# Spreading one operand of the graph-attention edge scores by DMA through DRAM instead of by matmuls, with the written order of one block changed to match

## Chip, cores and metric

The kernel runs on one core of a Trainium2 chip. The metric is device time in microseconds (us) of one launch, taken as the median of repeated runs. Beside it stands one profiled execution, whose trace and page are quoted here.

## What is computed

The input is 128 graphs of 128 nodes with 256 features each, and an adjacency matrix of zeros and ones for each graph. Layer 0 is a transformer layer with 8 heads, in which the attention probabilities are multiplied by value projections that depend on the edge's type. Layer 1 is two rounds of graph attention and a feed-forward block. All is in fp32.

```python
# layer 0
attn = softmax(q k^T / sqrt(32)); out = sum_r (attn * (adj == r)) @ v_r
x = LN(x + out @ Wo);  x = LN(x + gelu(x @ W1) @ W2)
# layer 1, twice _gat, then a feed-forward block
Wh  = h @ W;  Wh1 = Wh @ a[:F];  Wh2 = Wh @ a[F:]
e   = leaky_relu(Wh1 + transpose(Wh2))            # one number per pair of nodes
att = softmax(where(adj > 0, e, -9e15), axis=1);  h = att @ Wh
x = LN(x + h);  x = LN(x + relu(x @ w_ff1) @ w_ff2)
```

## The kernel before

The work is cut into 32 groups of four graphs (G = 4, 512 tokens). Everything of a group stays in SBUF. All weights are loaded once. A group goes through these stages; the names are those of the tiles in the profile.

- `projections`: `pq` gives q and k of the group (four steps), `pv` the values of each graph (four steps). ScalarE copies `qT` and `kT` out of PSUM, VectorE adds the bias to `v`.
- `attention`: `scores` computes `ps`, ScalarE takes Exp into `e`, VectorE masks it into `pm`; `attended` computes the denominators `pden` and the weighted values `pav`, and VectorE divides; then two output products `pwo`, each added to the residual by VectorE. A generator of five steps: scores 0; attended 0 with scores 1; attended 1; `pwo` 0; `pwo` 1.
- `ffn`: eight steps `ph` (two matmuls of 512 columns each, ScalarE applies Gelu or Relu into `hT`), then eight steps of `po` (eight matmuls of 256 columns each), sixteen steps in all. `first_ffn` belongs to layer 0, `second_ffn` to layer 1.
- `layer1`: the two rounds of graph attention. `pw` multiplies the group's input by `wu`, which holds W1 times W2 (256 columns) and the columns that give the score parts; ScalarE copies it to `wh`. The other score part has to stand along the free dimension on all 128 partitions. It is made there by a matmul with a weight of identical columns: `wb` in the first round (L480), and `wh`'s column D+1 broadcast to 128 columns in the second (L491). `edges` adds the two parts on ScalarE (L448, the `gs` activations with the column as bias), applies leaky relu on VectorE (L451), Exp on ScalarE (L452), the mask with its sums (L455), the reciprocal, and the division on GpSimd (L462). `py` is the first product with the scores, `pg2` (shown as `pg` in the profile) the second.
- `norm` is a layer norm (statistics and normalisation on VectorE, the power -1/2 and the scale and shift on GpSimd), `turned` transposes its result on TensorE (`pt`) and ScalarE copies it out to `yT`, `written` is the last norm and the output DMA.

Stages of three groups are interleaved by hand. `in_order(ffn_, *steps)` walks through its list: a number runs that many steps of the feed-forward block, a generator runs its next step, a function is called; what is left of the block runs at the end. In the loop over g there are two such lists: the first around `first_ffn` of group g+1 holds the beginning of `layer1` of group g; the second around `second_ffn` of group g holds the end of `layer1`, the projections and attention of group g+2, and the transposes. TensorE executes in the order written (`manual_schedule`). The order on the other engines is chosen by the scheduler when the kernel is built.

PSUM has eight buffers of 128x512: four in the pool `ps_s` (shared in turn by `ps`, `pt`, `pw`, `py` and `pg`), one each for `av` and `den`, two in `ps_mm` (`pq`, `pv`, `ph`, `po`, `pwo`). All loads of the loop and the output go through the DMA queue of SyncE (SP), in order.

Of the kernel before, what the change touches and what calls it, by code (L numbers as in the profile page):

```python
# [9 lines left out]
F32 = mybir.dt.float32  # L10
I32 = mybir.dt.int32
AF = mybir.ActivationFunctionType
# [11 lines left out]
P = 128  # L24
G = 4
T = G * P
# [77 lines left out]
def fast_pass(ctx, tc, a, out):  # L104
# [19 lines left out]
    w3p = ctx.enter_context(tc.tile_pool(name="work3", bufs=3))  # L124
    w1p = ctx.enter_context(tc.tile_pool(name="work1", bufs=1))
    small = ctx.enter_context(tc.tile_pool(name="small", bufs=4))
    ps_s = ctx.enter_context(tc.tile_pool(name="ps_s", bufs=4, space=PSUM))
    ps_av = ctx.enter_context(tc.tile_pool(name="ps_av", bufs=1, space=PSUM))
    ps_mm = ctx.enter_context(tc.tile_pool(name="ps_mm", bufs=2, space=PSUM))
# [69 lines left out]

    NU = D + 3
    wu = k.tile([P, NCH, NU], "wu")
    wb = k.tile([P, NCH, P], "wb")

    def graph_weights():

        scr = cut(D)
        wa1 = k.columns(gw1, a1, scr, "1")
        wa2 = k.columns(gw2, a2, scr, "2")  # L210
        rhs = cut(NCH, D + 2)
        nc.vector.tensor_copy(rhs[:, :, :D], gw2)
        nc.vector.tensor_copy(rhs[:, :, D : D + 1], wa2[:, :, 1:2])
        nc.vector.tensor_copy(rhs[:, :, D + 1 : D + 2], wa2[:, :, 0:1])
        gw1T = cut(NCH, D)
        for m in range(NCH):
            pt = mm_tile(f"pgt_{m}")
            for c in range(NCH):
                nc.tensor.transpose(
                    pt[:, c * P : (c + 1) * P], gw1[:, c, m * P : (m + 1) * P], k.ident  # L220
                )
            nc.scalar.copy(gw1T[:, m, :], pt[:, :D])
        yield
        for m in range(NCH):
            pu = mm_tile(f"pgw_{m}")
            for c in range(NCH):
                nc.tensor.matmul(
                    pu[:, : D + 2], gw1T[:, c, m * P : (m + 1) * P], rhs[:, c, :],
                    start=(c == 0), stop=(c == NCH - 1),
                )  # L230
            nc.scalar.copy(wu[:, m, : D + 2], pu[:, : D + 2])
            nc.vector.tensor_copy(wu[:, m, D + 2 :], wa1[:, m, 1:2])
            nc.vector.tensor_copy(wb[:, m, :], wa1[:, m, 0:1].to_broadcast([P, P]))

# [205 lines left out]
            added(t, p, po, S["xr"])  # L440
            yield

    def edges(pb, bias, S, l):

        n = f"{S['g']}_{l}"
        s = w2p.tile([P, G, P], F32, tag="gs", name="gs_" + n)
        for b in range(G):
            nc.scalar.activation(  # L448
                s[:, b, :], pb[:, b * P : (b + 1) * P], AF.Identity, bias=bias(b)
            )  # L450
        nc.vector.scalar_tensor_tensor(s, s, ALPHA, s, op0=ALU.mult, op1=ALU.max)  # L451
        nc.scalar.activation(s, s, AF.Exp)  # L452
        den = c_gat[:, S["g"], l, :]
        for b in range(G):
            nc.vector.scalar_tensor_tensor(  # L455
                s[:, b, :], s[:, b, :], 1.0, S["ad"][:, b, :],
                op0=ALU.mult, op1=ALU.mult, accum_out=den[:, b : b + 1],
            )
        rd = small.tile([P, G], F32, tag="gr", name="gr_" + n)
        nc.vector.tensor_scalar(rd, den, LO, None, op0=ALU.max)  # L460
        nc.vector.reciprocal(rd, rd)  # L461
        nc.gpsimd.tensor_mul(s, s, rd[:, :, None].to_broadcast([P, G, P]))  # L462
        return s

    def layer1(S):


        n, yT = str(S["g"]), S["x2T"]
        wh = w1p.tile([P, G, NU], F32, tag="wh", name="wh_" + n)
        for b in range(G):  # L470
            pw = ps_s.tile([P, T], F32, tag="s", name=f"pw_{n}_{b}")
            for c in range(NCH):
                nc.tensor.matmul(  # L473
                    pw[:, :NU], yT[:, c, b * P : (b + 1) * P], wu[:, c, :],
                    start=(c == 0), stop=(c == NCH - 1),
                )
            nc.scalar.copy(wh[:, b, :], pw[:, :NU])
        pb = ps_av.tile([P, T], F32, tag="den", name="pb_" + n)
        for c in range(NCH):
            nc.tensor.matmul(pb, wb[:, c, :], yT[:, c, :], start=(c == 0), stop=(c == NCH - 1))  # L480
        att = edges(pb, lambda b: wh[:, b, D + 2 : D + 3], S, 0)
        yield
        yh = w1p.tile([P, G, D + 1], F32, tag="yh", name="yh_" + n)
        pb = ps_av.tile([P, T], F32, tag="av", name="pb2_" + n)
        for b in range(G):
            py = ps_s.tile([P, T], F32, tag="s", name=f"py_{n}_{b}")
            nc.tensor.matmul(  # L487
                py[:, : D + 1], att[:, b, :], wh[:, b, : D + 1], start=True, stop=True
            )
            nc.scalar.copy(yh[:, b, :], py[:, : D + 1])  # L490
            nc.tensor.matmul(  # L491
                pb[:, b * P : (b + 1) * P], wh[:, b, D + 1 : D + 2].to_broadcast([P, P]),
                att[:, b, :], start=True, stop=True,
            )
        att = edges(pb, lambda b: yh[:, b, D : D + 1], S, 1)
        yield
        S["t2"] = t = w3p.tile([P, G, D], F32, tag="t", name="t_2_" + n)
        for p in range(G // 2):
            po = ps_s.tile([P, T], F32, tag="s", name=f"pg2_{n}_{p}")
            for s in range(2):  # L500
                b = 2 * p + s
                nc.tensor.matmul(  # L502
                    po[:, s * D : (s + 1) * D], att[:, b, :], yh[:, b, :D], start=True, stop=True
                )
            added(t, p, po, S["res1"])
        yield
# [44 lines left out]
    def first_ffn(S):  # L551
        yield from ffn(S, 1, S["x1T"], w1, b1, AF.Gelu, w2, S["res0"])

    def second_ffn(S):
        yield from ffn(S, 3, S["x3T"], u1, c1, AF.Relu, u2, S["res2"])
# [6 lines left out]

    with tc.manual_schedule(engines={mybir.EngineType.PE}):
        st = [first, entered(1)] + [None] * (NG - 2)
        none, steps = iter(()), graph_weights()
        at = attention(first)
        in_order(none, *[projections(first)] * 8, at, steps, at, steps, at, at, at)
        norm(first, 0)  # L570
        turned(first, 0)
        pr, at = projections(st[1]), attention(st[1])
        in_order(
            first_ffn(first), *[pr, 1] * 8, at, 2, at, 2, at, 2, at, at, lambda: norm(st[1], 0), 2
        )
        norm(first, 1)
        turned(st[1], 0)
        for g in range(NG - 1):
            S, S1 = st[g], st[g + 1]
            graph = layer1(S)  # L580
            if g + 2 < NG:
                st[g + 2] = S2 = entered(g + 2)
                if g == 0:
                    head = (4, lambda: turned(S, 1), 2)
                else:
                    head = (6,)
                in_order(
                    first_ffn(S1),
                    *(() if g == 0 else (lambda: written(st[g - 1]),)),
                    *head, graph, 6, graph, 4,  # L590
                )
                pr, at = projections(S2), attention(S2)
                norm(S1, 1, 0)
                in_order(
                    second_ffn(S), pr, pr, graph, lambda: norm(S, 2), lambda: norm(S1, 1, 1),
                    *[pr] * 6, lambda: turned(S1, 1), lambda: turned(S, 2),
                    at, 3, at, 3, at, 3, at, at, lambda: norm(S2, 0), 6, lambda: turned(S2, 0),
                )
            else:
                in_order(  # L600
                    first_ffn(S1), lambda: written(st[g - 1]),
                    graph, 5, graph, 5, graph, lambda: norm(S, 2), 5, lambda: turned(S, 2),
                )
                graph = layer1(S1)
                norm(S1, 1)
                in_order(
                    second_ffn(S), 4, lambda: turned(S1, 1), 1, graph, 5, graph, 5, graph,
                    lambda: norm(S1, 2),
                )
                written(S)  # L610
                turned(S1, 2)
                in_order(second_ffn(S1))
                written_by_graph(S1)
# [356 lines left out]
```

## Time and profile before

| | |
|---|---|
| median of 3 runs | 3107.01 us (3105.93 to 3108.55) |
| profiled execution | 3106.48 us, span 3104.7 us, granted TensorE clock 0.997 |
| TensorE busy | 3038.4 us (98%) |
| VectorE, ScalarE, GpSimd busy | 1349.4, 1077.0, 866.9 us |
| DMA | 69.59 MB, mean 22 GB/s |
| one group in the steady part | 95.67 us |

A row of a timeline gives the start and the length in us, the engine, the source line, the operation, the output and inputs by their names in the program, the shapes and the number of instructions; in brackets stands the idle time before it and what ended it. A matmul in fp32 has two records. Records of matmuls overlap, so a length is longer than the time until the next can start. A DMA row gives the number of issues, the size of each, and the median time from issue to landing. PE is TensorE, DVE VectorE, ACT ScalarE, POOL GpSimd.

### The profile page before, as it was taken

The page shows a single profiled execution, that of the slowest core. Times are in us where ns is not written, and L with a number is a line of the kernel's source. Part 1 is how long each engine was busy: PE and PEld are TensorE (multiplying, and loading weights), DVE is VectorE, ACT ScalarE, POOL GpSimd, SP SyncE. Part 2 cuts the span into 40 slices and gives each one's busy share as a digit, 9 for nine tenths or more (in the row PEclk, how much of TensorE's full clock was granted, in tenths as well). Part 3 has the DMA queues.
Part 4 walks back from the last instruction along what each step waited for, and adds up shares of the span by engine and source line. Part 5 has one row for each costly group of instructions (what it writes and reads, how often), then busy time and mean ns, then how long its engine had stood idle before and what let it go on. Part 6 is the DMA issues. An engine that isn't in the chain of part 4 may idle for free.

```text
span 3104.7 us, 39594 instructions
## 1 busy us (share of the span) xinstructions
PE 3038.4 (98%) x16526; PEld 1996.7 (64%) x16526; DVE 1349.4 (43%) x3445; ACT 1077.0 (35%) x1797; POOL 866.9 (28%) x489
## 2 busy tenths in 40 slices
PE   8999999999999999999999999999999999999998
PEld 4666666666666666666666666666666666666665
DVE  4544434444434454344444444443445434454443
ACT  2333343333433333333334333343333333333332
POOL 1223233232232322323313223223232232332322
PEclk9999999999999999999999999999999999999999
DMA  5000000000000000000000000000000000000000
GB/s 164 12 21 21 21 18 19 22 22 18 18 24 18 21 18 18 24 18 21 18 24 18 18 21 24 18 18 24 18 21 18 18 24 18 21 18 11 7 8 15
DMA packets 58137, 69.59 MB, mean 22 GB/s; under 512 B 6752, under 2 KB 44768, under 8 KB 57952
## 3 DMA queue, kind: packets, MB, share of 16 engines
q1 hardware_dynamic: 57120, 66.61, 7.0%
q8 instruction: 131, 2.15, 0.3%
q14 instruction: 54, 0.44, 0.0%
q10 hardware_dynamic: 832, 0.40, 0.0%
HBM read 50.22 MB, written 16.78 MB: 22 GB/s over the span
## 4 chain that ended last, share of the span: by engine, by line
PE 94%; ACT 3%; DVE 1%; DMA 1%; POOL 0%; SPq 0%; issue 0%; ACTq 0%; DVEq 0%; POOLq 0%
PE po L308 29%; PE ph L296 28%; PE pq L402 7%; PE pv L412 7%; PE pwo L436 4%; PE pw L473 4%; PE pav L372 3%; ACT yT L278 3%; PE ps L342 2%; PE pden L363 2%; PE py L487 2%; PE pb L480 2%; PE pg L502 2%; PE pt L275 2%; PE pb L491 1%; DVE t L285 1%
## 5 line engine op out<-in xcount | busy, mean ns | idle before, releaser
L255 POOL TENSOR_TENSOR rs<-rs,mhalf 128x4 f32<-128x4 f32 x127 | 128.9, 1015 | 1298.3 <-DVE rs L254 1298.2
L296 PE MATMUL ph<-yT,w_L_gnn_w_ff 128*128 128x512 f32 x1024 | 466.1, 603 | 0.0
L308 PE MATMUL po<-w_L_gnn_W,hT 128*128 128x256 f32 x2048 | 460.9, 381 | 1.3 <-ACT hT L300 1.3
L308 PE MATMUL po<-w_L_gnn_w_ff,hT 128*128 128x256 f32 x2048 | 457.5, 379 | 0.0
L296 PE MATMUL ph<-yT,w_L_gnn_W 128*128 128x512 f32 x1024 | 451.6, 592 | 2.4 <-ACT hT L300 2.0
L308 PEld LDWEIGHTS po<-w_L_gnn_W,hT 128*128 128x128 f32 x2048 | 384.0, 190 | 76.3 <-issue 14.5
L308 PEld LDWEIGHTS po<-w_L_gnn_w_ff,hT 128*128 128x128 f32 x2048 | 386.7, 190 | 65.1 <-issue 14.8
L296 PEld LDWEIGHTS ph<-yT,w_L_gnn_W 128*128 128x128 f32 x1024 | 194.2, 190 | 234.3 <-issue 219.8
L278 ACT ACTIVATE yT<-pt,c_L_gnn_beta,c_L_gnn_g 128x512 f32<-128x512 f32 x128 | 92.6, 773 | 721.6 <-PE pt L275 721.5
L296 PEld LDWEIGHTS ph<-yT,w_L_gnn_w_ff 128*128 128x128 f32 x1024 | 187.7, 190 | 215.2 <-issue 192.4
L285 DVE TENSOR_TENSOR t<-po,res 128x512 f32<-128x512 f32 x128 | 88.5, 691 | 445.7 <-PE po L308 445.7
L379 DVE RECIPROCAL rd<-pden 128x512 f32<-128x512 f32 x64 | 214.9, 3357 | 153.4 <-PE pden L363 153.3
L300 ACT ACTIVATE hT<-ph,c_L_gnn_b_ff 128x512 f32<-128x512 f32 x256 | 176.3, 689 | 291.9 <-PE ph L296 290.2
L462 POOL TENSOR_TENSOR gs<-gs,gr 128x512 f32<-128x512 f32 x64 | 66.5, 1039 | 724.1 <-DVE gr L461 712.9
L300 ACT ACTIVATE hT<-ph,c_L_gnn_b 128x512 f32<-128x512 f32 x256 | 175.7, 687 | 219.2 <-PE ph L296 218.7
L412 PE MATMUL pv<-wv,xT 128*128 128x512 f32 x512 | 225.4, 592 | 0.0
L451 DVE SCALAR_TENSOR_TENSOR gs<-gs 128x512 f32<-128x512 f32 x64 | 44.6, 697 | 412.9 <-ACT gs L448 412.8
L350 DVE TENSOR_TENSOR pm<-e,adj 128x512 f32<-128x512 f32 x256 | 159.5, 685 | 130.5 <-ACT e L349 130.5
L251 DVE BATCH_NORM_STATS2 st<-t 128x6 f32<-128x256 f32 x508 | 192.3, 415 | 7.4
L257 DVE TENSOR_SCALAR t<-t,mv,rs 128x256 f32<-128x256 f32 x384 | 132.6, 409 | 112.5 <-POOL rs L255 112.5
L349 ACT ACTIVATE e<-ps 128x512 f32<-128x512 f32 x256 | 132.1, 603 | 140.5 <-PE ps L342 140.5
L412 PEld LDWEIGHTS pv<-wv,xT 128*128 128x128 f32 x512 | 97.3, 190 | 122.4 <-issue 122.2
(110 smaller groups left out, 3772.1 us busy)
## 6 DMA issues: line engine op xcount, KB each, us to landing
xT<-in_xT_dram SPq DMA_DIRECT2D x32, 512.0 KB, 3.6
x<-in_x_dram SPq DMA_DIRECT2D x32, 512.0 KB, 3.9
out_dram<-t SPq DMA_DIRECT2D x31, 512.0 KB, 2.9
adj<-in_adjT_dram SPq DMA_DIRECT2D x32, 256.0 KB, 2.7
w_L_gnn_W<-in_L_gnn_W_dram SPq DMA_DIRECT2D x2, 1024.0 KB, 7.6
w_L_gnn_w_ff<-in_L_gnn_w_ff_dram SPq DMA_DIRECT2D x2, 1024.0 KB, 9.9
wv<-in_L_gnn_Wv_dram SPq DMA_DIRECT2D x2, 256.0 KB, 5.3
temp<-in_L_gnn_W_dram SPq DMA_DIRECT2D x2, 256.0 KB, 4.9
```

The lines of the kernel that those rows point to most:

```text
L251: nc.vector.bn_stats(st[:, b, :], t[:, b, :])
L255: nc.gpsimd.tensor_tensor(rs, rs, k.mhalf, op=ALU.pow)
L257: nc.vector.tensor_scalar(t[:, b, :], t[:, b, :], mv[:, b, 0:1], rs[:, b : b + 1], op0=ALU.subtract, op1=ALU.mult,)
L278: nc.scalar.activation(yT[:, c, :], pt, AF.Identity, bias=bc[:, c : c + 1], scale=gc[:, c : c + 1])
L296: nc.tensor.matmul(ph, wa[:, c, f * P : (f + 1) * P], inT[:, c, :], start=(c == 0), stop=(c == NCH - 1),)
L300: nc.scalar.activation(hT[:, f, :], ph, func, bias=ba[:, f : f + 1])
L308: nc.tensor.matmul(po[:, s * D : (s + 1) * D], hT[:, f, b * P : (b + 1) * P], wb_[:, f, :], start=(f == 0), stop=(f == NF - 1),)
L349: nc.scalar.activation(e[:, s], pss[s], AF.Exp, scale=SCALE)
L350: nc.vector.tensor_mul(pm[:, s], e[:, s], ad[:, 2 * p : 2 * p + 2, None, :].to_broadcast([P, 2, NCH, P]),)
L379: nc.vector.reciprocal(rd, pden)
L402: nc.tensor.matmul(pq, w[:, c, m * P : (m + 1) * P], xt[:, c, :], start=(c == 0), stop=(c == NCH - 1),)
L412: nc.tensor.matmul(pv, xt[:, c, b * P : (b + 1) * P], wv[:, c].rearrange("p r d -> p (r d)"), start=(c == 0), stop=(c == NCH - 1),)
```

## The change

The broadcast matmuls L480 and L491 and the tile `wb` are removed. `wu` gets a fourth extra column, so that `pw` delivers both score parts as columns of `wh`, and `py` delivers both as columns of `yh`. A new function `spread` takes one column per graph (128 partitions x 4), writes it by DMA to a small DRAM tile `line` (four rows of 128 numbers), and reads it back by a second DMA into all 128 partitions, as the SBUF tile `pb` (128x512). Both DMAs go on SP's queue. `edges` reads `pb` from SBUF.

`layer1` now has five steps instead of three: `pw` with the first transfer; edges 0; `py` with the second transfer; edges 1; `pg2`. The lists of `in_order` put feed-forward steps or projections between them. In the second list the transposes `turned(S1, 1)` and `turned(S, 2)`, which stood together ahead of scores 0, are put one v product ahead of them and two v products behind them, and one `ph` step stands between the two `pwo`. ScalarE is added to the engines that execute in written order.

```diff
-    NU = D + 3
+    NU = D + 4
     wu = k.tile([P, NCH, NU], "wu")
-    wb = k.tile([P, NCH, P], "wb")
...
-            nc.vector.tensor_copy(wb[:, m, :], wa1[:, m, 0:1].to_broadcast([P, P]))
+            nc.vector.tensor_copy(wu[:, m, D + 2 : D + 3], wa1[:, m, 1:2])
+            nc.vector.tensor_copy(wu[:, m, D + 3 :], wa1[:, m, 0:1])
...
+    def spread(column, n):
+        line = dram.tile([G, P], F32, tag="line", name="line_" + n)
+        with nc.allow_non_contiguous_dma(reason="a column per graph as a row"):
+            nc.sync.dma_start(line.rearrange("b p -> p b"), column)
+        pb = w2p.tile([P, G, P], F32, tag="pb", name="pb_" + n)
+        nc.sync.dma_start(pb, line.partition_broadcast(P))
+        return pb
...
-        pb = ps_av.tile([P, T], F32, tag="den", name="pb_" + n)
-        for c in range(NCH):
-            nc.tensor.matmul(pb, wb[:, c, :], yT[:, c, :], start=(c == 0), stop=(c == NCH - 1))
-        att = edges(pb, lambda b: wh[:, b, D + 2 : D + 3], S, 0)
+        target = spread(wh[:, :, D + 3], n + "_0")
         yield
-        yh = w1p.tile([P, G, D + 1], F32, tag="yh", name="yh_" + n)
-        pb = ps_av.tile([P, T], F32, tag="av", name="pb2_" + n)
+        att = edges(target, wh[:, :, D + 2 : D + 3], S, 0)
+        yield
+        yh = w1p.tile([P, G, D + 2], F32, tag="yh", name="yh_" + n)
         for b in range(G):
...
-            nc.tensor.matmul(
-                pb[:, b * P : (b + 1) * P], wh[:, b, D + 1 : D + 2].to_broadcast([P, P]),
-                att[:, b, :], start=True, stop=True,
-            )
-        att = edges(pb, lambda b: yh[:, b, D : D + 1], S, 1)
+            nc.scalar.copy(yh[:, b, :], py[:, : D + 2])
+        target = spread(yh[:, :, D + 1], n + "_1")
+        yield
+        att = edges(target, yh[:, :, D : D + 1], S, 1)
         yield
...
-    with tc.manual_schedule(engines={mybir.EngineType.PE}):
+    with tc.manual_schedule(engines={mybir.EngineType.PE, mybir.EngineType.Activation}):
...
                 else:
-                    head = (6,)
+                    head = (1,)
                 in_order(
                     first_ffn(S1),
                     *(() if g == 0 else (lambda: written(st[g - 1]),)),
-                    *head, graph, 6, graph, 4,
+                    *head, graph, 7, graph, 4, graph, 4,
                 )
...
                 in_order(
-                    second_ffn(S), pr, pr, graph, lambda: norm(S, 2), lambda: norm(S1, 1, 1),
-                    *[pr] * 6, lambda: turned(S1, 1), lambda: turned(S, 2),
-                    at, 3, at, 3, at, 3, at, at, lambda: norm(S2, 0), 6, lambda: turned(S2, 0),
+                    second_ffn(S), graph, *[pr] * 4, graph, lambda: norm(S, 2), lambda: norm(S1, 1, 1),
+                    pr, lambda: turned(S1, 1), pr,
+                    at, pr, pr, lambda: turned(S, 2),
+                    at, 4, at, 3, at, 1, at, lambda: norm(S2, 0), 6, lambda: turned(S2, 0),
                 )
...
                 in_order(
                     first_ffn(S1), lambda: written(st[g - 1]),
-                    graph, 5, graph, 5, graph, lambda: norm(S, 2), 5, lambda: turned(S, 2),
+                    graph, 3, graph, 3, graph, 3, graph, 3, graph, lambda: norm(S, 2),
+                    4, lambda: turned(S, 2),
                 )
...
                 in_order(
-                    second_ffn(S), 4, lambda: turned(S1, 1), 1, graph, 5, graph, 5, graph,
+                    second_ffn(S), 4, lambda: turned(S1, 1), 1,
+                    graph, 3, graph, 3, graph, 3, graph, 2, graph,
                     lambda: norm(S1, 2),
                 )
```

More of the change, by code (lines that the diff above doesn't have):

```diff
@@ L126, in fast_pass @@
     small = ctx.enter_context(tc.tile_pool(name="small", bufs=4))
+    dram = ctx.enter_context(tc.tile_pool(name="dram", bufs=2, space=bass.MemoryType.DRAM))
     ps_s = ctx.enter_context(tc.tile_pool(name="ps_s", bufs=4, space=PSUM))
@@ L231, in graph_weights @@
             nc.scalar.copy(wu[:, m, : D + 2], pu[:, : D + 2])
-            nc.vector.tensor_copy(wu[:, m, D + 2 :], wa1[:, m, 1:2])
-            nc.vector.tensor_copy(wb[:, m, :], wa1[:, m, 0:1].to_broadcast([P, P]))
+            nc.vector.tensor_copy(wu[:, m, D + 2 : D + 3], wa1[:, m, 1:2])
+            nc.vector.tensor_copy(wu[:, m, D + 3 :], wa1[:, m, 0:1])
     c_adj = k.tile([P, NG], "c_adj")
@@ L441, in attention, with edges @@
             yield
-    def edges(pb, bias, S, l):
+    def spread(column, n):
[5 more added lines that the diff above has]
+        return pb
+    def edges(target, source, S, l):
         n = f"{S['g']}_{l}"
@@ L448, in edges @@
             nc.scalar.activation(
-                s[:, b, :], pb[:, b * P : (b + 1) * P], AF.Identity, bias=bias(b)
+                s[:, b, :], target[:, b, :], AF.Identity, bias=source[:, b, :]
             )
@@ L487, in layer1 @@
             nc.tensor.matmul(
-                py[:, : D + 1], att[:, b, :], wh[:, b, : D + 1], start=True, stop=True
+                py[:, : D + 2], att[:, b, :], wh[:, b, : D + 2], start=True, stop=True
             )
-            nc.scalar.copy(yh[:, b, :], py[:, : D + 1])
-            nc.tensor.matmul(
-                pb[:, b * P : (b + 1) * P], wh[:, b, D + 1 : D + 2].to_broadcast([P, P]),
-                att[:, b, :], start=True, stop=True,
-            )
-        att = edges(pb, lambda b: yh[:, b, D : D + 1], S, 1)
+            nc.scalar.copy(yh[:, b, :], py[:, : D + 2])
+        target = spread(yh[:, :, D + 1], n + "_1")
+        yield
+        att = edges(target, yh[:, :, D : D + 1], S, 1)
         yield
@@ L573, in fast_pass @@
         in_order(
-            first_ffn(first), *[pr, 1] * 8, at, 2, at, 2, at, 2, at, at, lambda: norm(st[1], 0), 2
+            first_ffn(first), *[pr, 1] * 8, at, 2, at, 2, at, 2, at, 1, at, lambda: norm(st[1], 0), 1
         )
@@ L583, in fast_pass @@
                 if g == 0:
-                    head = (4, lambda: turned(S, 1), 2)
+                    head = (4, lambda: turned(S, 1), 1)
                 else:
-                    head = (6,)
+                    head = (1,)
                 in_order(
```

## Prediction

> **What bounds the kernel now.** I read the busy shares first, then the chain that ended last, then the timeline of one steady group (it repeats every 95.67 us: the 48-matmul stretch of L308 starts at 190.40, 286.07, 381.75).
>
> ```profile
> PE 3038.4 (98%) x16526; PEld 1996.7 (64%) x16526; DVE 1349.4 (43%) x3445; ACT 1077.0 (35%) x1797; POOL 866.9 (28%) x489
> PE 94%; ACT 3%; DVE 1%; DMA 1%; POOL 0%; SPq 0%; issue 0%; ACTq 0%; DVEq 0%; POOLq 0%
> ```
>
> TensorE is both the busiest engine and 94% of the chain, so an instruction that leaves its queue shortens the run by its start-to-start time, and an edit elsewhere counts only where TensorE comes to wait. The timeline of TensorE shows what the change touches (start, length, group):
>
> ```profile
> 1019.70 1.91 PE L275 MATMUL pt<-ident,t 128*128 128x128 f32 x16
> 1021.54 0.78 PE L342 MATMUL ps<-qT,kT 32*128 32x128 f32 x4
> 1022.50 0.48 PE L342 MATMUL ps<-qT,kT 32*128 32x128 f32 x2 [0.18 <-ACT yT L278]
> 1023.17 1.15 PE L342 MATMUL ps<-qT,kT 32*128 32x128 f32 x26 [0.18 <-ACT yT L278]
> 1024.26 5.42 PE L296 MATMUL ph<-yT,w_L_gnn_w_ff 128*128 128x512 f32 x12
> ...
> 1046.80 1.89 PE L436 MATMUL pwo<-w_L_gnn_Wo,oT 128*128 128x256 f32 x8
> 1049.48 1.99 PE L436 MATMUL pwo<-w_L_gnn_Wo,oT 128*128 128x256 f32 x8 [0.78 <-DVE t L285]
> ...
> 1078.07 1.88 PE L480 MATMUL pb<-yT,wb 128*128 128x512 f32 x4
> 1079.79 3.60 PE L296 MATMUL ph<-yT,w_L_gnn_W 128*128 128x512 f32 x8
> ...
> 1090.81 0.38 PE L491 MATMUL pb<-gs,wh 128*128 128x128 f32 x2
> 1091.03 0.60 PE L487 MATMUL py<-wh,gs 128*128 128x257 f32 x2
> ```
>
> Records overlap, so I use differences of starts, not lengths. The score matmuls take 2.72 us (1021.54 to 1024.26) although the other batch of the same 32 takes 1.10 (1032.35 to 1033.45): they wait for the PSUM buffers of the transposes just ahead, which ScalarE is still emptying. The chain gives that stretch to "ACT yT L278", 2.79 us, so the printed 0.18 understates it.
>
> The cover for the new transfers is judged by these rows:
>
> ```profile
> adj<-in_adjT_dram SPq DMA_DIRECT2D x32, 256.0 KB, 2.7
> out_dram<-t SPq DMA_DIRECT2D x4, 128.0 KB, 1.8
> 1073.81 0.38 SPq L527 DMA_DIRECT2D out_dram<-t  x1
> 1093.28 1.14 ACT L448 ACTIVATE gs<-pb,yh 128x128 f32<-128x128 f32 x4
> 1095.73 0.63 ACT L452 ACTIVATE gs<-gs 128x512 f32<-128x512 f32 x1
> 1097.89 1.04 POOL L462 TENSOR_TENSOR gs<-gs,gr 128x512 f32<-128x512 f32 x1 [10.98 <-DVE gr L461]
> ```
>
> The last three are one edge chain: 5.65 us from the first gs to the normalised scores (1093.28 to 1098.93), with a table load of 1.28 inside.
>
> [...] 4-byte packets of the column loads at the start take 8 to 9 ns each, and some 1,084 of them pass in 1.9 us. [...]
>
> **The change, part by part** (per steady group unless said).
>
> (a) Broadcast matmuls removed: L480, 1079.79-1078.07 = 1.72 us; L491, four times 1091.03-1090.81 = 0.22, 0.88. In all 2.60 x 32 groups = -83.2 us. wb's copies (0.4 us in all) were hidden anyway.
>
> (b) One more column in pw (259 to 260) and py (257 to 258): 24 records at 0.43 us per 512 columns, under 1 ns each: 0.02 us a group, +0.6.
>
> (c) Transposes away from the scores: two v products now follow scores 0, and turned(S, 2) comes after them. The transposes of turned(S1, 1) have one v product (1.72 us) between them and scores 0; ScalarE's two copies end about 1.3 us after the last transpose (773 ns each). The wait of 2.72-1.10 = 1.62 goes, 30 groups: -48.6. If the cover failed it would be the same 1.62 again.
>
> (d) pwo: one ph product now stands between its halves. Before, the second half started 2.68 us after the first instead of 1.73; -0.95 x 31 = -29.5. The next one late would be DVE's add (0.69 + 0.2), inside 1.72.
>
> (e) ScalarE in written order, edges after the last hT: Gelu's table is no longer swapped out amid hT. "PEld po L308 <- ACT hT L300" is 14.2 us over 32 waits; its effect on starts is 7.16 against 6.91 us per 32 records, -0.25 x 31 = -7.7.
>
> (f) First transfer. Take t = 0 at the group's first ph. pw ends at 5.2 (ph 1.72, four pw 3.50), the last wh copy at 5.8 (0.2 behind it, 0.38 long). SP's queue has the output write of the group before ahead of it, issued 9.5 us after that ph (1073.81-1064.27); so the line goes at 9.95, lands about a microsecond behind those 512 KB (2.9 from issue), at 13.5, and the broadcast 2.7 later, at about 16.3. gs stands behind the last hT (ph ends at 5.2+7 x 1.717 = 17.2, then 0.2+0.69), at 18.05: 1.7 us of slack. Scores ready at 18.05+5.65 = 23.7; py is due at 17.2 + 4 steps of 1.73 = 24.1. Cost 0, slack 0.4; without that cover the trip costs what it passes 8.1 by. Behind the waiting gs stand Exp and the yh copies, which nothing needs before py. The wh copies also wait for the last group's line to be read, long done.
>
> (g) Second transfer. py ends (call it 0), yh at 0.6. Trip D: the write 2.3 (1.8 of the 128 KB row, plus 512 pieces at 1.9/1084), the broadcast 2.7 (adj's row: same 128 packets of 2 KB), 0.1 between: D = 5.1. Bounds: 4.5 (1.8 + 2.7), and 7 if 4-byte writes cost twice the reads and 128 reads of one 2 KB row slow the broadcast. gs starts at 0.6+D, takes 1.15. On DVE the normalisation of t1 is queued between the masked sums and the reciprocal (order of instructions in the changed kernel) and waits for POOL's power: leaky relu and Exp 1.4, sums and statistics 1.7, power 1.13 (rs to L257), normalisation 1.38, reciprocal 0.45, POOL's product 1.2, hand-over 0.1 make 7.35 us from the last gs to the scores on TensorE, so ready at 9.1+D. TensorE gets to pg at 13.8 (4 po steps 6.9, four q/k products 6.87). Slack is 4.7-D = -0.4: about 0.5 x 30 = +15 (0 to 70). Behind gs on ScalarE stand Exp and the q copies; these hold up the third q/k product only from D = 6.5.
>
> (h) SP: adj, xT, x come behind these four issues; they wait for releases at about 39, 51 and 76 us anyway and are used a group or more later. 0. DVE and POOL get no work. ScalarE reads its gs from SBUF instead of PSUM, the same 128 columns: 0.
>
> (i) Last two groups: only three ffn steps (5.2 us) lie between graph stages, and in group 31's turn the read-back stands behind an output write. Edges block hT there: in group 30 gs can start at about 14, and Exp and the reload of Gelu put the fourth hT at 18.6, where TensorE wants its buffer at 12.1 (6.5); pg then waits some 2.4, and in group 31 py 0.7 and pg 3.5. Less the 1.96 and 1.29 that ph and po wait there now: +10 (0 to 20).
>
> Sum: -83.2+0.6-48.6-29.5-7.7+15+10 = -143. From the profiled run's 3106.5 us (span 3104.7), which lies 0.5 below the median of 3107.0: **2963**. The group would go from 95.67 to some 90.8.
>
> **Rivals.**
> 1. Two round trips do not fit. In both stages DMA becomes the wait. Second stage costs D-4.7, first D-8.1; (a) to (e) less (i) give about 5.3 per group, so it turns slower where (D-4.7)+(D-8.1) passes 5.3: **D = 9**. At D = 12 it is +11.2-5.3 = 5.9 x 30: about 3280. Against it: no steady transfer of 256 or 512 KB takes over 3.9 us; for it: column loads at the crowded start took up to 9.3, and 4-byte writes to DRAM are nowhere in the trace.
> 2. The trip is late by some more (D 6 to 8), or small slacks of 0.3 to 0.5 us (scores 0, py, v's PSUM) fail: 1 to 4 us a group come back, 3000 to 3080.
> 3. The moves do nothing, as another buffer is late in place of (c) and (d): only (a) is left less the trip, -83+25: about 3050.
>
> **How the numbers follow.** Forecast 0.57 (range 2940 to 2995); rivals 2 and 3 together 0.31; rival 1 0.10; the rest about no change. A measurement of this kernel can tell 0.2% (6 us) from nothing. Faster 0.87, same 0.03, slower 0.10. The range must reach into rivals 2 and 3: 2935 to 3065 leaves out rival 1, the upper end of 2, and a little below.
>
> **What would show it.** Right: no row pb<- on PE, TensorE busy down by about 80 us, ps after pv at 1.1 us a batch, no pwo wait, period near 90.8, pg waiting a few tenths for POOL. Wrong: "ACT gs <- DMA pb" followed by PE waiting for POOL gs by microseconds a group (rival 1 or 2); ps or pwo still waiting (rival 3). The landing times of line and pb give D directly; a line write of over 4 us would break the forecast.

## The result, and the profile after

The changed kernel takes 3756.4 us (median of 4 runs, 3754.34 to 3758.12) against 3107.66 (3105.93 to 3108.55): a ratio of 1.2088, with an interval of 1.2067 to 1.2109. It is 21% slower. The forecast was 2963, so the result lies on the other side of no change and outside the range. The profiled execution has a span of 3752.5 us and a granted TensorE clock of 0.911.

The busy shares of the changed kernel, and the shares of its chain by engine:

```profile
PE 3153.6 (84%) x16142; PEld 2055.3 (55%) x16142; DVE 1568.4 (42%) x3445; ACT 1011.6 (27%) x1735; POOL 906.4 (24%) x489
...
PE 49%; DMA 24%; DVE 16%; POOL 6%; ACT 4%; issue 2%; SPq 1%; ACTq 0%; POOLq 0%
```

TensorE was 94% of the chain and is now 49%. Its busy time has grown although 384 records of matmuls are gone, and VectorE is busy for 219 us more (1349.4 before) with the same number of instructions. So two things need an explanation, and DMA is only one of them. The table of waits (engine, line, what it waited for; total, times, longest, in us):

```profile
ACT gs L457 <- DMA pb<-line: 605.5, 64, 13.3
...
PE pq L402 <- DVE t L285: 212.9, 29, 7.7
...
PE py L495 <- POOL gs L471: 171.5, 31, 8.5
...
PE pav L372 <- DVE pm L350: 140.6, 62, 2.3
```

The first three belong to the two transfers. The fourth does not: `pm`, the mask of the attention scores, touches nothing of what the change spreads. The landing times of the DMA issues:

```profile
pb<-line SPq DMA_DIRECT2D x64, 256.0 KB, 4.6
out_dram<-t SPq DMA_DIRECT2D x31, 512.0 KB, 4.9
...
line<-wh SPq DMA_DIRECT2D x32, 2.0 KB, 9.2
line<-yh SPq DMA_DIRECT2D x32, 2.0 KB, 8.2
```

The write of 2 KB takes 8 to 9 us, twice as long as the 256 KB read-back behind it. In the second trip the two together are 12.8 us (the prediction's D was 5.1). The timeline of one steady group (start and length in us; in brackets the idle time before the row and what ended it), with the two trips:

```profile
1044.56 0.38 SPq L533 DMA_DIRECT2D out_dram<-t  x1
...
1044.99 0.50 SPq L447 DMA_DIRECT2D line<-wh  x1
...
1052.25 7.07 PE L308 MATMUL po<-w_L_gnn_W,hT 128*128 128x256 f32 x32
...
1055.88 0.33 SPq L449 DMA_DIRECT2D pb<-line  x1
1059.26 1.28 ACT L457 ACTIVATE gs<-pb,wh 128x128 f32<-128x128 f32 x4 [6.12 <-DMA pb<-line]
...
1065.11 3.68 PE L495 MATMUL py<-wh,gs 128*128 128x258 f32 x8 [5.79 <-POOL gs L471]
...
1069.22 0.36 SPq L447 DMA_DIRECT2D line<-yh  x1
...
1075.53 1.88 PE L402 MATMUL pq<-xT,w_L_gnn_Wq 128*128 128x512 f32 x4
...
1077.28 0.33 SPq L449 DMA_DIRECT2D pb<-line  x1
1081.96 1.27 ACT L457 ACTIVATE gs<-pb,yh 128x128 f32<-128x128 f32 x4 [12.76 <-DMA pb<-line]
1083.27 0.69 DVE L460 SCALAR_TENSOR_TENSOR gs<-gs 128x512 f32<-128x512 f32 x1 [13.68 <-ACT gs L457]
1083.88 0.68 DVE L285 TENSOR_TENSOR t<-po,res 128x512 f32<-128x512 f32 x1
...
1084.62 3.78 PE L402 MATMUL pq<-xT,w_L_gnn_Wq 128*128 128x512 f32 x4 [7.20 <-DVE t L285]
```

In the first trip `py` waits 5.79 us. In the second, TensorE does not wait for the scores at all; it stops at the second half of `pq`. That half needs the PSUM buffer of `po`, which VectorE frees with its add L285; the add stands in VectorE's queue behind `gs` L460, and `gs` waits for ScalarE, which waits for the DMA. The rest of the loss stands behind the scores:

```profile
1098.17 1.17 PE L342 MATMUL ps<-qT,kT 32*128 32x128 f32 x32
1099.27 3.70 PE L412 MATMUL pv<-wv,xT 128*128 128x512 f32 x8
...
1107.98 0.41 PE L372 MATMUL pav<-pm,v 128*32 128x128 f32 x2 [2.34 <-DVE pm L350]
...
1110.72 0.42 PE L372 MATMUL pav<-pm,v 128*32 128x128 f32 x1 [2.34 <-DVE pm L350]
...
1113.85 2.09 PE L342 MATMUL ps<-qT,kT 32*128 32x128 f32 x32
...
1131.13 1.89 PE L436 MATMUL pwo<-w_L_gnn_Wo,oT 128*128 128x256 f32 x8
1132.86 1.88 PE L296 MATMUL ph<-yT,w_L_gnn_w_ff 128*128 128x512 f32 x4
1134.58 1.89 PE L436 MATMUL pwo<-w_L_gnn_Wo,oT 128*128 128x256 f32 x8
```

The moves did what they were meant to do: `ps` passes in 1.10 us (1098.17 to 1099.27) without a wait for the transposes, and neither `pwo` half waits. But `pav` waits twice for `pm`. VectorE and GpSimd at the same moment:

```profile
1099.50 2.36 POOL L265 TENSOR_TENSOR res<-t,r_L_gnn_g_ln 128x1024 f32<-128x1024 f32 x1 [1.50 <-DVE t L257]
1099.99 10.68 DVE L350 TENSOR_TENSOR pm<-e,adj 128x512 f32<-128x512 f32 x4
1101.82 2.81 POOL L265 TENSOR_TENSOR res<-t,r_L_gnn_g 128x1024 f32<-128x1024 f32 x1
...
1104.59 2.78 POOL L266 TENSOR_TENSOR res<-res,r_L_gnn_b_ln 128x1024 f32<-128x1024 f32 x1
1107.34 2.78 POOL L266 TENSOR_TENSOR res<-res,r_L_gnn_beta 128x1024 f32<-128x1024 f32 x1
```

Four `pm` take 10.68 us, 2.7 each, and last until GpSimd's scale and shift (`scaled`, L265 and L266) are through. In the kernel before, `pm` took 0.68 (678 to 693 ns), and GpSimd had finished at 1023.9, just before `pm` began at 1024.8:

```profile
1021.54 2.36 POOL L266 TENSOR_TENSOR res<-res,r_L_gnn_beta 128x1024 f32<-128x1024 f32 x1
1024.79 2.50 DVE L350 TENSOR_TENSOR pm<-e,adj 128x512 f32<-128x512 f32 x4 [4.20 <-ACT e L349]
```

### The profile page after: what moved, and what is told of

The parts are those of the page before. It is cut to its first block, busy times and chain, and to the rows that moved or that the text cites. A ratio compares the mean times of both kernels' runs of the same rounds, so it can differ in the third digit from the quotient of the medians.

```text
span 3752.5 us, 39020 instructions
## 1 busy us (share of the span) xinstructions
PE 3153.6 (84%) x16142; PEld 2055.3 (55%) x16142; DVE 1568.4 (42%) x3445; ACT 1011.6 (27%) x1735; POOL 906.4 (24%) x489
## 4 chain that ended last, share of the span: by engine, by line
PE 49%; DMA 24%; DVE 16%; POOL 6%; ACT 4%; issue 2%; SPq 1%; ACTq 0%; POOLq 0%
PE ph L296 14%; PE po L308 12%; DVE pm L350 9%; DMA line<-wh 8%; DMA line<-yh 7%; DMA pb<-line 7%; PE pq L402 6%; PE pav L372 4%; PE py L495 3%; PE pwo L436 3%; ACT gs L457 2%; PE pw L483 2%; POOL t L265 2%; POOL t L266 2%; PE ps L342 2%
## 5 line engine op out<-in xcount | busy, mean ns | idle before, releaser
L460 DVE SCALAR_TENSOR_TENSOR gs<-gs 128x512 f32<-128x512 f32 x64 | 44.3, 692 | 1107.4 <-ACT gs L457 1107.4
L308 PE MATMUL po<-w_L_gnn_W,hT 128*128 128x256 f32 x2048 | 455.7, 380 | 0.0
L308 PE MATMUL po<-w_L_gnn_w_ff,hT 128*128 128x256 f32 x2048 | 452.4, 379 | 0.0
L308 PEld LDWEIGHTS po<-w_L_gnn_W,hT 128*128 128x128 f32 x2048 | 394.5, 193 | 69.7 <-issue 15.0
L308 PEld LDWEIGHTS po<-w_L_gnn_w_ff,hT 128*128 128x128 f32 x2048 | 386.9, 190 | 52.3 <-issue 1.0
L350 DVE TENSOR_TENSOR pm<-e,adj 128x512 f32<-128x512 f32 x256 | 405.1, 1640 | 4.7 <-ACT e L349 4.7
L402 PE MATMUL pq<-xT,w_L_gnn_Wq 128*128 128x512 f32 x256 | 178.5, 837 | 219.2 <-DVE t L285 212.9
L372 PE MATMUL pav<-pm,v 128*32 128x128 f32 x2048 | 188.1, 330 | 140.6 <-DVE pm L350 140.6
L495 PE MATMUL py<-wh,gs 128*128 128x258 f32 x256 | 115.8, 630 | 171.5 <-POOL gs L471 171.5
L412 PE MATMUL pv<-wv,xT 128*128 128x512 f32 x512 | 238.6, 598 | 0.0
L402 PEld LDWEIGHTS pq<-xT,w_L_gnn_Wq 128*128 128x128 f32 x256 | 61.8, 256 | 294.6 <-DVE t L285 236.9
```

Source lines behind the costliest of these rows:

```text
L308: nc.tensor.matmul(po[:, s * D : (s + 1) * D], hT[:, f, b * P : (b + 1) * P], wb_[:, f, :], start=(f == 0), stop=(f == NF - 1),)
L350: nc.vector.tensor_mul(pm[:, s], e[:, s], ad[:, 2 * p : 2 * p + 2, None, :].to_broadcast([P, 2, NCH, P]),)
L372: nc.tensor.matmul(pav[s * DH : (s + 1) * DH, u, c, :], v[:, d0 : d0 + DH], m[:, s, u, c, :], start=(r == 0), stop=(r == 1),)
L402: nc.tensor.matmul(pq, w[:, c, m * P : (m + 1) * P], xt[:, c, :], start=(c == 0), stop=(c == NCH - 1),)
L412: nc.tensor.matmul(pv, xt[:, c, b * P : (b + 1) * P], wv[:, c].rearrange("p r d -> p (r d)"), start=(c == 0), stop=(c == NCH - 1),)
L495: nc.tensor.matmul(py[:, : D + 2], att[:, b, :], wh[:, b, : D + 2], start=True, stop=True)
```

## Experiments

**Theories.** T1: the round trip through DRAM is too slow and is the whole loss. T2: beside it the new order puts GpSimd's `scaled` on top of VectorE's `pm`; this costs some 7 us a group and has nothing to do with the trip. Below, "period" is the mean distance from one group's first `pw` to the next, over groups 5 to 25: 95.67 us before, 116.05 after.

**1. The new order without the trips** (`order_only`).

```diff
...
-        target = spread(wh[:, :, D + 3], n + "_0")
+        target = ps_av.tile([P, G, P], F32, tag="den", name="pb_" + n)
+        for c in range(NCH):
+            nc.tensor.matmul(
+                target, wb[:, c, :], yT[:, c, :], start=(c == 0), stop=(c == NCH - 1)
+            )
...
+        target = ps_av.tile([P, G, P], F32, tag="av", name="pb2_" + n)
...
-        target = spread(yh[:, :, D + 1], n + "_1")
+            nc.tensor.matmul(
+                target[:, b, :], wh[:, b, D + 1 : D + 2].to_broadcast([P, P]),
+                att[:, b, :], start=True, stop=True,
+            )
```

> The changed kernel's orders and transposes are kept, but the target part of the scores is spread by the matmuls of the kernel before (wb, pb in ps_av) and takes no round trip through DRAM. T1 (the round trip costs about 13 us of each group directly, and that alone is the loss): all of the loss goes and the moves bring what the prediction gave them, so about 3020 us (3107 less 2.6 to 2.8 us on each of 30 groups). T2 (about 7 us of each group is a collision on VectorE and GpSimd, pm beside scaled, that the new order makes by itself): no ScalarE gs waits for a DMA and no py waits for gs, but pm stays at 1.5 us or more on the mean and PE's pav waits some 6 to 7 us a group for it, so about 3220 to 3300 us, slower than the kernel before.

3262.92 us, ratio 1.0494 (1.0477 to 1.0512), period 100.69. There are no trips in this kernel, and it is still 5% slower than the one before. T1 alone falls.

**2. The trips without the collision** (`gated`). GpSimd copies one number out of the last `pm` into the tile that it is about to write, so that its scaling waits for `pm`. The two calls for the scaling are moved behind the score steps whose `pm` they wait for.

```diff
-            S[f"res{i}"] = scaled(S[f"t{i}"], *rows[i], n)
+            o = None
+            if pm is not None:
+                o = w3p.tile([P, G, D], F32, tag="res", name="res_" + n)
+                nc.gpsimd.tensor_copy(o[:, G - 1, D - 1 : D], pm[:, HC - 1, 1, NCH - 1, P - 1 : P])
+            S[f"res{i}"] = scaled(S[f"t{i}"], *rows[i], n, o)
...
```

> The changed kernel with its round trips, but GpSimd's scaling of a group's second half waits until VectorE's pm of head 0 are done, and that of its first half until those of head 1 are done, so the two do not overlap. T1 (round trip alone): the time stays within 1% of 3756 us, since pm was only slow in the shadow of another wait. T2 (collision adds to it): pm is back at 0.68 us on the mean, the pav waits go, and the time falls by 7 to 9 us on each of 30 groups, to about 3490 to 3550 us; the waits of gs for pb and of py for gs stay.

3566.23 us, 190 less than the changed kernel, period 109.39. The group of `pm` in the changed kernel (after the bar its busy time in us and the mean of one in ns):

```profile
L350 DVE TENSOR_TENSOR pm<-e,adj 128x512 f32<-128x512 f32 x256 | 405.1, 1640 | 4.7 <-ACT e L349 4.7
```

and in this kernel:

```profile
L350 DVE TENSOR_TENSOR pm<-e,adj 128x512 f32<-128x512 f32 x256 | 159.6, 685 | 4.7 <-ACT e L349 4.7
```

The overlap makes `pm` slow, as T2 has it. The time is 16 us above the expected range: the two stretches behind `pm` give back all of their 8.45 us a group, but the two trips cost 1.6 more than in the changed kernel (the landings of `line` have medians of 10.0 and 8.9 us here, against 9.2 and 8.2), which leaves a gain of 6.66. Why they land later here is not shown.

**3. Nothing to spread** (`const_pb`), and **the same without the collision** (`const_gated`).

Both leave out the target part of the edge scores: a tile of zeros, written once, stands for it.

```diff
+    pbc = k.tile([P, G, P], "pbc")
+    nc.vector.memset(pbc, 0.0)
...
-        line = dram.tile([G, P], F32, tag="line", name="line_" + n)
...
-        return pb
+        return pbc
```

> Leaves out the target part of the edge scores (a tile of zeros stands for it), and so every line written and every pb read; all else is the changed kernel. T1: what is left is the schedule as predicted, a period of about 90 us and 2940 to 2960 us. T2: the collision of pm and scaled stays, so about 3160 to 3230 us, with no wait of ScalarE for a DMA. The difference between this time and 3756 us is the round trips' whole cost, by T2 about 530 to 600 us (17 to 19 us a group).

> Leaves out the target part of the edge scores as before (zeros stand for it), with GpSimd's scaling held back. This is the schedule of the prediction with a round trip that costs nothing: its sum without the 15 us for the second trip gives about 2950 us (period about 90 us); if more than the collision was wrong in the prediction of the schedule, 2990 us or more.

3182.95 us (1.0239, 1.0219 to 1.026; period 98.14), and 2944.35 us (0.9472, 0.9455 to 0.9489; period 90.16). The last one is the schedule of the prediction with a trip that costs nothing. The prediction's sum is 2948 without (g), and 2938 without (i) as well. So the schedule on TensorE was right, and everything lost lies in the trips and the collision. Alone, the collision costs 239 us (3183 - 2944) and the trips 622 (3566 - 2944); together 812 (3756 - 2944), 49 less than the sum.

**4. The restored matmuls without the collision** (`order_gated`).

> The changed kernel's orders and transposes with the broadcast matmuls of the kernel before in place of the round trips, and with GpSimd's scaling held back until pm of a head are done. T2 (the collision is all that spoils the moves): pm at 0.68 us, no pav wait, so 3263 us less 7 to 8 us on each of 30 groups, 3020 to 3045 us, 2 to 3% faster than the kernel before. If the moves themselves bring nothing (the prediction's rival 3): 3085 to 3110 us.

3028.12 us, ratio 0.9742 (0.9729 to 0.9755), period 92.77. Against the kernel before, only the order and the extra column are changed here, and `scaled` is held back; this brings 2.90 us a group.

**5. Larger pieces** (`packed`). The column is first gathered into a tile of four columns; DRAM gets 128 pieces of 16 bytes. The read-back then delivers the four graphs' numbers in turn, so ScalarE reads `pb` with a step of four (four `gs` take 1.75 us in a row of `packed_gated` below, 1.28 in the changed kernel).

```diff
-        line = dram.tile([G, P], F32, tag="line", name="line_" + n)
...
-            nc.sync.dma_start(line.rearrange("b p -> p b"), column)
...
+        pk = small.tile([P, G], F32, tag="pk", name="pk_" + n)
+        nc.vector.tensor_copy(pk, column)
+        line = dram.tile([P, G], F32, tag="line", name="line_" + n)
+        nc.sync.dma_start(line, pk)
...
```

> The changed kernel, but the column goes to DRAM as 128 pieces of 16 bytes instead of 512 pieces of 4 bytes (VectorE copies it once to a tile of 4 columns, pb is read back whole and ScalarE reads it with a stride). If the time to landing is set by the number of pieces (T1a: 8 to 9 us for 512), line lands in 3.5 to 5 us, D falls from 12.7 to about 8 or 9 us, and the time falls by about 4 us on each of two trips, to about 3480 to 3560 us. If a write to DRAM lands late whatever its pieces (T1b), line still takes 8 to 9 us and the time stays within 1.5% of 3756 us. In both, pm stays slow beside scaled.

3256.33 us, ratio 1.0477 (1.0459 to 1.0494), period 99.85: 500 us less than the changed kernel for the same bytes. The expected gain was too small, because both parts of the trip became faster; the second trip has a median of 5.9 us, not 8 or 9. The landing times of this kernel:

```profile
pb<-line SPq DMA_DIRECT2D x64, 256.0 KB, 3.5
out_dram<-t SPq DMA_DIRECT2D x31, 512.0 KB, 3.7
...
line<-pk SPq DMA_DIRECT2D x64, 2.0 KB, 2.4
```

With the collision removed as well (`packed_gated`):

> The changed kernel with both mends: pieces of 16 bytes and GpSimd's scaling held back. With the round trip at about 6 us and no collision: 3256 us less 7 to 8 us on each of 30 groups, 3015 to 3050 us. If the collision was hiding part of the trip (the trips now end later than the time that the faster schedule leaves them), up to 3100 us, with a wait of PE's pq for VectorE's t of 2 to 4 us a group.

3025.74 us, ratio 0.9733 (0.9719 to 0.9746), period 92.16. The added copy shows the collision in its plainest form. It moves 128x4 numbers; the first time while GpSimd works, the second time while it is idle (timeline of `packed_gated`):

```profile
1229.58 2.35 POOL L265 TENSOR_TENSOR t<-t,r_L_gnn_g_ln 128x1024 f32<-128x1024 f32 x1 [1.55 <-PE pw L487]
1230.67 1.29 DVE L446 COPY pk<-wh 128x4 f32<-128x4 f32 x1 [1.22 <-ACT wh L491]
...
1251.63 0.17 DVE L446 COPY pk<-yh 128x4 f32<-128x4 f32 x1 [0.75 <-ACT yh L502]
```

The first copy ends at 1231.96, as GpSimd's instruction does (1231.93). It did not run slowly, it was held until the other had ended: in all 29 groups in which the copy begins while GpSimd's L265 runs, it ends 22 to 30 ns after that instruction, also in the one group where more of it is left and the copy takes 1.59 us. `pm` keeps to GpSimd's ends in the same way: 120 of the 256 in the changed kernel run beside a GpSimd instruction and take 2.41 to 2.87 us, and each of these ends 545 to 553 ns behind one of GpSimd's; the other 136 take 0.68 to 0.69. Not every VectorE instruction is held. In the kernel before, 121 of the 128 `v` (with one input in PSUM) run beside GpSimd, and all 128 take 0.69 us; one of them runs from 1018.18 although GpSimd's L265 runs from 1016.92 to 1019.27. What decides which instruction is held is not shown.

**6. What makes the write late** (`probes`). `order_gated` with one write per group that nobody reads, issued where `line` is, in four shapes by turns.

> order_gated with one DMA to DRAM added per group that nobody reads, in four shapes by turns: 512 pieces of 4 bytes turned into rows (line0, the changed kernel's write), 512 pieces of 4 bytes that lie side by side as in the tile (line1), 512 pieces of 16 bytes (line2), 128 pieces of 16 bytes (line3). T1a (the number of pieces sets the landing): line0, line1 and line2 land in 8 to 9 us, line3 in 2.4. T1c (the size of a piece, 4 bytes, does): line0 and line1 late, line2 in 2.5 to 3. T1d (the turned order of addresses does, neighbours in DRAM being written by different partitions): line0 alone is late. The time stays that of order_gated within 0.5%.

3027.31 us, the time of `order_gated`. Landing, eight samples each:

| shape | KB | median us | lowest to highest |
|---|---|---|---|
| 512 pieces of 4 bytes, turned into rows (the change's) | 2 | 10.6 | 8.9 to 13.1 |
| 512 pieces of 4 bytes, in order | 2 | 8.2 | 7.8 to 9.5 |
| 512 pieces of 16 bytes, in order | 8 | 4.2 | 3.6 to 4.8 |
| 128 pieces of 16 bytes | 2 | 1.4 | 1.4 to 2.4 |

The size of a piece decides most: at the same number of pieces, four times the bytes land in half the time (4.2 us instead of 8.2). The turned order adds some 2 us (10.6 instead of 8.2). The last row can't be compared directly, since that probe needs only the first `wh` copy and was issued ahead of the output write. The same shape behind the output write, in `hybrid` below, takes 3.3, so by an estimate from these two the number of pieces (512 against 128 of 16 bytes) is worth about 1 us (4.2 less 3.3). What the 4-byte writes wait for stays open: in the changed kernel's trace the packets of the second trip's write, issued at 1069.22, pass between 1070.1 and 1070.5 us, and it lands at 1077.3. No earlier write stands just ahead of it in the queue, so waiting behind the output is not the reason there.

**7. Where packed_gated still loses 81 us** (`late`). The second `gs` stage stands one projection step later in the written order, and with it `pg` and the scaling behind it; the cut below is against `packed_gated`.

```diff
...
-                    second_ffn(S), graph, *[pr] * 4, graph, lambda: norm(S, 2, 0),
-                    pr, lambda: turned(S1, 1), pr,
+                    second_ffn(S), pr, graph, *[pr] * 4, graph, lambda: norm(S, 2, 0),
+                    lambda: turned(S1, 1), pr,
...
```

> packed_gated with the graph's second score step (edges of layer 1 in the code's count) put one projection batch later in the written order, so that VectorE's t of po_1 and ScalarE's qT stand ahead of gs in their queues. In packed_gated the trip still costs 3026 - 2944 = 82 us against the kernel without it, and PE's pq waits 26 us for t; if the rest (56 us) is this same queue at work (ScalarE's qT behind gs, VectorE's norm pieces between gs, matmuls that run slower after each short stall), most of it goes: 2950 to 2975 us, 4 to 5% faster than the kernel before. If the trip costs by something else (its traffic, ScalarE's slower strided read of pb, the added copy on VectorE), only the 26 us go: 2995 to 3005 us. If pg now waits for gs: 3015 us or more.

3026.88 us: no gain. The number lies where the expectation puts it if `pg` waits for `gs`, but that wait is gone (9.8 us in all in `packed_gated`, 2.1 here), so the reason is another. TensorE's costliest wait for another engine in the steady groups of `packed_gated`:

```profile
PE pq L402 <- DVE t L285: 26.0, 29, 1.7
```

and in those of `late`:

```profile
PE pq L402 <- ACT qT L406: 40.8, 30, 6.1
```

The wait on VectorE's queue is gone, and one on ScalarE's has taken its place: now `qT` stands behind `gs` and Exp, and the next `pq` lacks its buffer. A late `gs` holds up VectorE's queue in the one order (26.0 us of waits) and ScalarE's in the other (40.8).

**8. One trip each** (`hybrid`, `hybrid4`). The second spread goes back to the `pb2` matmuls. The first stays a DMA, in 16-byte pieces (`hybrid`) or as in the change (`hybrid4`). Both hold `scaled` back.

> packed_gated with the second round trip only given back to the matmuls of the kernel before (pb2 beside py); the first one stays a DMA of 128 pieces of 16 bytes. If the first trip is hidden at a landing of about 6 us and the 82 us of packed_gated are the second trip's: the py phase is 0.89 us longer per group than without broadcast matmuls (2.63 against 1.74 us), so 2944 + 32 x 0.89 = 2970 to 2980 us, 4 to 4.5% faster than the kernel before. If the cost is spread over both trips (traffic, slower reads of pb by ScalarE): 3000 us or more.

> The same with the first round trip written as in the changed kernel, 512 pieces of 4 bytes, which land in 8 to 10 us. If the two trips of the changed kernel cost about the same (py waits 6 to 7 us a group for the first, pq 8 us for the second, each with a slow stretch of PE behind it): 2975 us plus 8 to 10 us on each of 31 groups, 3220 to 3290 us. If the first trip's lateness is made up later in the group: under 3150 us.

2990.69 us, ratio 0.9617 (0.9603 to 0.963), period 91.36; and 3266.29 us, ratio 1.0509 (1.0493 to 1.0525), period 100.17. In 16-byte pieces the first trip is hidden in the steady part: the period is 1.20 us above `const_gated`, of which 0.99 is the `py` stage with `pb2` in it and 0.2 a wait of `py`. (The 11 us above the expected range are about that wait and the last groups.) In 4-byte pieces the same trip costs 8.81 us a group more than that, with `py` waiting 211.1 us in all. `hybrid` is the fastest kernel here with the whole computation, 3.8% faster than the kernel before.

## Why the prediction was wrong, step by step

Here is where the period went, from the starts on TensorE in the changed kernel (the group shown above) against the same stretches of a group of `const_gated`, which takes 90.16 us:

| stretch | after | without trips and collision | lost |
|---|---|---|---|
| `po` to `py` (first trip) | 12.86 | 6.91 | 5.95 |
| `py` to the second `po` | 3.51 | 1.74 | 1.77 |
| `pq` to `pg` (second trip) | 16.51 | 6.87 | 9.64 |
| last `pt` to scores 1 (`pm`) | 11.04 | 3.71 | 7.33 |
| scores 1 and the `ph` behind it | 12.03 | 10.91 | 1.12 |
| sum | | | 25.81 of 25.89 |

- **(a) and (b), matmuls removed: right.** `order_gated` less `const_gated` is 2.61 us a group; (a) predicted 2.60. Both have the extra column of (b), which shows only in `pw`: 3.51 us after, 3.50 before.
- **(c), (d), (e), the moves: right.** 1.62 + 0.95 + 0.25 = 2.82 a group were predicted; 95.67 - 92.77 = 2.90 were measured once the collision was out of the way. The `ps`, `pwo` and `po` rows are as foreseen.
- **(f), first trip at no cost: wrong by its duration alone.** The line was issued 9.98 us after the first `ph` (9.95 predicted), but landed 10.89 later instead of 3.5, and `gs` began at 24.25 instead of 18.05. The rule, that the trip costs what it passes 8.1 by, held: 14.27 - 8.1 = 6.2, against 5.95 in the table. With 16-byte pieces the trip fitted, as the step said.
- **(g), second trip at D = 5.1: wrong twice.** D was 12.76 here (median 13.0), outside the step's bounds of 4.5 to 7 (the 7 was the author's assumption). The write's 2.3 us were put together from a 128 KB write of large pieces and from column *loads*, whose 4-byte packets take 8 to 9 ns each; a write in 4-byte pieces had no row in the trace, and its landing is what counts. (The sum has a slip too: 1.8 and 512 x 1.9/1084 make 2.7, so D would be 5.5, still far from 12.76.) A trip in 16-byte pieces has a median of 5.9, near the step's figure. Second, the step looked for the loss at `pg` and for queued work on ScalarE alone. It fell on `pq`, through VectorE's add of `po`, which stood behind `gs`. That queue bites at a D near 5 by an estimate (5.9 less 0.9), not at 6.5: in `packed_gated`, with a median D of 5.9, `pq` waits 26.0 us over 29 groups, 0.9 each, and in one group with a D of 6.45 it waits 1.38.
- **(h), "DVE and POOL get no work. 0": wrong, by 239 us where nothing else is late.** The amount of work did stay the same. But the moves shifted when `pm` and `scaled` run against each other, and the step never set the two side by side, though their times could be read from the trace of before. Rival 3 looked for a failing move only in a buffer that comes late.
- **(i), the last groups at +10: too small.** From the first `pw` of the last steady group to the end it took 212.3 us before, 222.2 in `order_gated`, 212.2 in `const_gated`, 232.6 in `packed_gated` and 278.9 after. So the new order by itself costs about the 10 us that were foreseen (222.2 - 212.3); against `const_gated`, trips with a D of 5.9 add 20 us, and the changed kernel has 67 more.
- **Left out: TensorE's pace behind a stall.** After the 7.20 us wait, four records of `pq` take 3.78 instead of 1.88; after 5.79, eight of `py` take 3.68 instead of 1.90; scores 1, behind the `pav` waits, take 2.09 instead of 1.17. The trace records the granted clock (the number behind the engines' busy times is PEclk; this is the group shown above):

```profile
core 0: us, PE busy (x) PEld busy (x) DVE busy (x) ACT busy (x) POOL busy (x), PEclk, DMA share, GB/s
1058.30:1061.71 3.41, 1.02 (x5) 0.56 (x3) 0.69 (x1) 2.43 (x5) 0.00 (x0) 1.00 0.06 17
1061.71:1065.11 3.40, 0.01 (x1) 0.01 (x1) 2.50 (x13) 0.76 (x2) 1.04 (x1) 0.50 0.00 0
1065.11:1068.54 3.43, 3.43 (x8) 2.78 (x9) 0.34 (x3) 1.12 (x3) 0.00 (x0) 0.50 0.00 0
1068.62:1075.53 6.91, 6.91 (x33) 6.08 (x32) 0.70 (x2) 0.37 (x1) 0.00 (x0) 1.00 0.04 0
1084.62:1089.02 4.40, 4.40 (x5) 1.85 (x6) 3.40 (x19) 1.16 (x2) 1.02 (x1) 0.50 0.23 63
1106.09:1109.50 3.41, 0.41 (x2) 0.14 (x2) 3.41 (x2) 0.00 (x0) 3.41 (x2) 1.00 0.01 4
1110.72:1116.32 5.60, 5.59 (x83) 4.77 (x84) 5.60 (x7) 0.36 (x1) 0.00 (x0) 0.50 0.01 3
```

The slow stretches are those at half clock. In `const_gated`, where nothing stalls, the same `py` stage has it whole:

```profile
1039.11:1040.85 1.74, 1.74 (x10) 1.52 (x9) 1.51 (x5) 0.99 (x3) 0.00 (x0) 1.00 0.00 0
```

All changes of the granted clock in this trace stand whole multiples of 3.413 us apart, so the 3.41 us before a fall are compared here. They need not be idle: the clock fell at 1061.71, after 3.41 us in which TensorE had been busy for 1.02, and again at 1109.50, between the two `pav` waits of 2.34, after 3.41 us with 0.41 busy. At the 69 falls between 200 and 2900 us of this trace TensorE had been busy for 1.11 at most in the 3.41 us before; in the 585 such stretches at full clock that no fall followed, for 1.74 at least. What else sets the clock is not shown. TensorE worked 3.43, 4.40 and 5.59 us of this group at half clock. At the full one the same work takes about half of that (`py` 1.74 in the row above instead of 3.43, four records of `pq` 1.88 instead of 3.78), so by an estimate, half the sum of the three, 6.7 of the 25.9 us are the clock's. They are contained in the rows of the table: 1.77 in `py`, 2.2 in `pq`, the rest in `pav`, scores 1 and the first of the `ph` behind it.

Rival 1 had the right sign and the right mechanism for most of the loss, and its mark, "a line write of over 4 us", came true. It gave 3280 at D = 12. `gated`, which is that rival alone, took 3566: the second trip had a median of 14.0 us there and the first, from the issue of the write to `gs`, 15.0, which by the rival's own sum makes 10.9 us a group, or about 3430; behind these stalls the matmuls also took about twice as long (`py` 3.61 to 3.81 us instead of 1.90, the second half of `pq` 3.51 to 3.78 instead of 1.88), and the last groups took 278.8 us instead of 212.3. A chance of 0.10 was too little for a step whose only relevant row, the 4-byte write, did not exist in the trace. Two readings were slightly off without bearing on this: single steady loads of 512 KB take up to 4.1 us (3.9 is the median of one of them), and the three starts of L308 are 190.24, 285.91 and 381.58, with the same distance.

## What to carry to other kernels

When a stage is moved, write down not only the engine that waits, but which VectorE and GpSimd instructions will then run at the same time; an order that is right on TensorE lost 8 us of each group to one such pair (98.14 against 90.16), and one dependence of a single number gave it back. Judge a DMA by its time to landing in the same direction and with the same piece size, and gather scattered 4-byte numbers on chip before writing them: one small copy, with the larger pieces that it allows, took 500 us off this kernel. Behind an engine that waits for a transfer, look through every queue, and ask which of them frees a PSUM buffer.

## What was not expected of the hardware

- 2 KB written to DRAM in 4-byte pieces land in 8 to 10 us, and 8 KB in as many pieces of 16 bytes in 4.2. The packets of the 4-byte write issued at 1069.22 pass in 0.4 us; it lands 6.8 us later.
- A VectorE copy of 128x4 numbers took 1.29 us instead of 0.17, because it ended only with the GpSimd instruction beside it; `pm` went from 0.68 to 2.7 us, and GpSimd's own instructions only from 2.36 to 2.8.
- The read-back of `line` landed in a median of 4.6 us behind the 4-byte writes and 3.5 behind the 16-byte ones, with the same 256 KB; the output write went from 4.9 to 3.7.
- The granted TensorE clock fell to half after stretches that were not idle throughout: once after 3.41 us with 1.02 us of matmuls in them, once, between two waits of 2.34 us, after 3.41 us with 0.41.
